# A scan's main loop written out in a fixed order, with POOL's decay operands made one step earlier

## The chip, the cores and the metric

The kernel runs on one core of a Trainium2 chip. The metric is device time in microseconds (us); the time of a kernel is the median of its runs. A profile is one further execution, recorded instruction by instruction; its span is the time from the first to the last recorded instruction.

The engines are named as in the profile: PE multiplies matrices (PEld is its loading of weights), DVE and POOL work elementwise on vectors, ACT applies functions, SP issues the DMAs. Each engine takes its instructions strictly in the order of its own queue; an instruction that waits holds up all that stand behind it on the same engine.

## The reference, cut to what matters

Three parts follow one another: a graph attention, a scan in the manner of Mamba-2, and a feed-forward part with quantized and low-rank weights. The change is in the scan:

```python
h = x * rsqrt(mean(x * x)) * norm_w
proj = einsum('bsd,od->bso', h, in_proj_w)          # gate, hidden, B, C, dt
hBC = silu(causal_conv(hBC, conv_w, conv_b))        # 4 taps along the sequence
hid_dt = hid * dt
M = einsum('bcihn,bcjhn->bcijh', Ch, Bh) * L        # L = exp(segsum(A * dt))
Y_diag = einsum('bcijh,bcjhp->bcihp', M, hid_dt)
y = (Y_diag + D_res) * silu(gate)                   # D_res = Dp * hid
ygr = y * rsqrt(mean over a group of 1024 channels of y * y)
out = residual + einsum('bsd,od->bso', ygr * gnorm_w, out_proj_w)
```

There are 16 sequences of 32 steps (512 tokens), 128 heads of 64 channels (8192 inner channels) and 8 groups. A sequence of 32 fits into one chunk, so that only Y_diag is computed.

## The kernel before, in words

**Tiling.** The 8192 inner channels are 64 tiles `t` of 128 channels, 8 tiles (`TG`) to each of the 8 groups (`G_M`). A tile is 128 channels by 512 tokens, in float32; one matmul of 512 columns shows as two records in the trace.

**The steps of a tile.** `project` (L1181) loads a weight block by a DMA on SP (`win`, 6 buffers) and runs four matmuls into a PSUM tile of a pool with two buffers. For the gate the result is `ppg`, and ACT makes `gs` from it (L1260). For the hidden channels it is `ppch`; `convolve` lets ACT make the first tap `cyh` (L1188), DVE add three taps (L1193), and ACT apply silu to give `hid` (L1196). This is `inner(g)`.

`mix(g)` then takes each tile: PE transposes `hid` into `pht` (L1289); DVE multiplies by `dt` into `hd` (L1291); for every second tile `decays` lets POOL make the operand `da` (L1269), PE sum it into `pl` (L1274) and ACT take the exponential `ed` (L1279); DVE multiplies two `el` (L1302) from `ed` and `CB`; PE multiplies `py` (L1310, 16 records); DVE adds and gates (`hid` L1314, `gs` L1315); ACT squares (`sq`, L1320), POOL adds the squares into `ssq` (L1321), and ACT scales `gs` (L1322).

`close(g)` sums `ssq` on PE (`pn`, L1329), makes the reciprocal root `gr` on ACT and DVE (L70 to L80, L1331), loads eight blocks `wo` of the output weights (L1337) and multiplies them with `gs`: four PSUM tiles `po` of eight matmuls (L1342), in a pool with two buffers; each is scaled and added to `xt` on DVE (L1345).

**Side work.** `lows.load` is a generator of ten chunks for the feed-forward part's low-rank weights: it clears its tiles on POOL (L179), issues nine small DMAs a chunk (L185), and splits a chunk on DVE one step later (`split`, L161 to L173). `inner(g)` for g > 0 takes one step of it after each tile.

**The order.** The source calls `inner(g + 1)`, `mix(g)`, `close(g)`, group by group. But this is not the order in the queues: in the scan a scheduler places the instructions of each engine, and it mixes `close(g)`'s matmuls into those of `mix(g)`, moves most projections of group g + 1 ahead of the mix, and puts ten `wo` loads at the very start of the scan. In the graph part a fixed order of the source holds (`manual_schedule`).

Of the kernel before, what the change touches and what calls it, by code (L numbers as in the profile page):

```python
# [8 lines left out]
F32 = mybir.dt.float32  # L9
# [3 lines left out]
AF = mybir.ActivationFunctionType  # L13
ALU = mybir.AluOpType
# [4 lines left out]
P = 128  # L19
B = 16  # L20
C = 32
D = 512
# [9 lines left out]
CB = 3  # L32
# [8 lines left out]
H_M, G_M, SEQ = 128, 8, 32  # L41
D_INNER = 8192
NT = D_INNER // P
TG = NT // G_M
# [9 lines left out]
def kernel(ctx: ExitStack, tc: tile.TileContext, I, out):  # L54
# [69 lines left out]
    with ExitStack() as cx:  # L124
        scan_part(nc, tc, cx, I, id32, ones, xt, U, rstd, lows)
# [4 lines left out]
class LowRank:  # L130
# [985 lines left out]
def scan_part(nc, tc, cx, I, id32, ones, xt, u, rstd, lows):  # L1116
# [50 lines left out]
    for q in range(4):  # L1167
        pt = ps_m.tile([P, 4, P], F32, tag="m", name=f"pt{q}")
# [6 lines left out]
    def project(t, tag):  # L1175

        w = wpool.tile([P, 4, P], F32, tag="win", name=f"win{tag}", bufs=6)
        nc.sync.dma_start(out=w, in_=I["in_proj"][t])
        pp = ps_p.tile([P, D], F32, tag="p", name=f"pp{tag}")
        for k in range(4):  # L1180
            nc.tensor.matmul(pp, lhsT=w[:, k], rhs=hT[:, k], start=(k == 0), stop=(k == 3))  # L1181
        return pp

    def convolve(dst, t, tag):

        pp = project(NT + t, f"c{tag}")
        y = wk.tile([P, B, SEQ], F32, tag="cy", name=f"cy{tag}", bufs=3)
        nc.scalar.activation(  # L1188
            y.rearrange("p b s -> p (b s)"), pp, AF.Identity, bias=cb[:, t:t + 1], scale=cw[:, t, 3:4]
        )  # L1190
        pv = pp.rearrange("p (b s) -> p b s", b=B)
        for sh in (1, 2, 3):
            nc.vector.scalar_tensor_tensor(  # L1193
                y[:, :, sh:], pv[:, :, :SEQ - sh], cw[:, t, 3 - sh:4 - sh], y[:, :, sh:], ALU.mult, ALU.add
            )
        nc.scalar.activation(dst, y.rearrange("p b s -> p (b s)"), AF.Silu)  # L1196


    wdt = wpool.tile([P, 4, P], F32, tag="win", name="wdt", bufs=6)
# [36 lines left out]
    CB = sc.tile([P, G_M, 4, P], F32, name="CB")  # L1236
# [13 lines left out]
    parts = lows.load(low)  # L1250
    big = cx.enter_context(tc.tile_pool(name="sbig", bufs=2))

    def inner(g):

        gs = big.tile([P, TG, D], F32, tag="gs", name=f"gs{g}")
        hid = big.tile([P, TG, D], F32, tag="hid", name=f"hid{g}")
        for i in range(TG):
            t = g * TG + i
            pg = project(t, f"g{t}")
            nc.scalar.activation(gs[:, i], pg, AF.Silu)  # L1260
            convolve(hid[:, i], t, f"h{t}")
            if g > 0:
                next(parts, None)
        return gs, hid

    def decays(h):

        da = sm.tile([P, 4, 4, SEQ], F32, tag="da", name=f"da{h}", bufs=2)
        nc.gpsimd.tensor_tensor(  # L1269
            da, lei.unsqueeze(1).unsqueeze(1).to_broadcast([P, 4, 4, SEQ]),  # L1270
            dA[:, :, h:h + 4].rearrange("p q h -> p h q").unsqueeze(3).to_broadcast([P, 4, 4, SEQ]), ALU.mult,
        )
        pl = ps_m.tile([P, 4, 4, SEQ], F32, tag="m", name=f"pl{h}")
        nc.tensor.matmul(  # L1274
            pl.rearrange("p h q i -> p (h q i)"), lhsT=gt, rhs=da.rearrange("p h q i -> p (h q i)"),
            start=True, stop=True,
        )
        ed = sm.tile([P, 4, 4, SEQ], F32, tag="ed", name=f"ed{h}", bufs=2)
        nc.scalar.activation(ed, pl, AF.Exp)  # L1279
        return ed  # L1280

    def mix(g, gs, hid):

        ssq = wk.tile([P, D], F32, tag="ssq", name=f"ssq{g}")
        for i in range(TG):
            t = g * TG + i
            pt = ps_m.tile([P, 4, P], F32, tag="m", name=f"pht{t}")
            for q in range(4):
                nc.tensor.transpose(pt[:, q], hid[:, i, q * P:(q + 1) * P], id32)  # L1289
            hd = sm.tile([P, 4, 2, 64], F32, tag="hd", name=f"hd{t}")  # L1290
            nc.vector.tensor_tensor(  # L1291
                hd, pt.rearrange("p q (h c) -> p q h c", h=2),
                dt[:, :, 2 * t:2 * t + 2].unsqueeze(3).to_broadcast([P, 4, 2, 64]), ALU.mult,
            )
            py = ps_y.tile([P, 4, P], F32, tag="y", name=f"py{t}")
            if i % 2 == 0:
                decay = decays(2 * t)
            els = []
            for j in range(2):

                el = sm.tile([P, 4, P], F32, tag="el", name=f"el{2 * t + j}")
                nc.vector.tensor_tensor(  # L1302
                    el.rearrange("p q (b i) -> p q b i", b=4),
                    decay[:, 2 * (i % 2) + j].unsqueeze(2).to_broadcast([P, 4, 4, SEQ]),
                    CB[:, g].rearrange("p q (b i) -> p q b i", b=4), ALU.mult,
                )
                els.append(el)
            for q in range(4):
                for j in range(2):
                    nc.tensor.matmul(  # L1310
                        py[64 * j:64 * j + 64, q], lhsT=hd[:, q, j], rhs=els[j][:, q], start=True, stop=True
                    )
            pyf = py.rearrange("p q t -> p (q t)")
            nc.vector.scalar_tensor_tensor(hid[:, i], hid[:, i], dpc[:, t:t + 1], pyf, ALU.mult, ALU.add)  # L1314
            nc.vector.tensor_tensor(gs[:, i], gs[:, i], hid[:, i], ALU.mult)  # L1315
# [7 lines left out]
        return ssq  # L1323

    def close(g, gs, ssq):
# [8 lines left out]
        wo = []  # L1334
        for i in range(TG):
            w = wpool.tile([P, D], F32, tag="wo", name=f"wo{g}_{i}", bufs=TG + 2)
            nc.sync.dma_start(out=w, in_=I["out_proj"][g * TG + i])  # L1337
            wo.append(w)
        for q in range(4):
            po = ps_o.tile([P, D], F32, tag="o", name=f"po{g}_{q}")  # L1340
            for i in range(TG):
                nc.tensor.matmul(  # L1342
                    po, lhsT=gs[:, i, q * P:(q + 1) * P], rhs=wo[i], start=(i == 0), stop=(i == TG - 1)
                )
            nc.vector.scalar_tensor_tensor(xt[:, q], po, rs[:, q:q + 1], xt[:, q], ALU.mult, ALU.add)  # L1345

    cur = inner(0)
    for g in range(G_M):
        nxt = inner(g + 1) if g + 1 < G_M else None
        ssq = mix(g, *cur)  # L1350
        close(g, cur[0], ssq)
        cur = nxt


def ffn_part(nc, tc, cx, I, id32, xt, layernorm, lows, out):
# [139 lines left out]
```

## Time and profile before

| what | value |
|---|---|
| time, median of 3 runs | 2353.34 us (2352.94 to 2354.5) |
| the profiled execution's own time | 2354.35 us |
| its span | 2352.6 us |
| mean granted TensorE clock | 0.981 |
| first `ppg` matmul | 1402.1 us |
| last `xt` addition of the scan (start) | 2253.48 us |

The main loop of the scan thus lies between 1402 us and 2254 us, 36% of the span. Within it the page's groups give (records, busy time):

| line, engine | what | records | busy us |
|---|---|---|---|
| L1181 PE | `ppg` and `ppch` | 1024 | 464.1 |
| L1342 PE | `po` | 512 | 240.5 |
| L1310 PE | `py` | 1024 | 90.6 |
| L1289 PE | `pht` | 256 | 41.9 |
| L1274 PE | `pl` | 64 | 34.3 |
| L1302 DVE | `el` | 128 | 107.8 |
| L1321 POOL | `ssq` | 56 | 80.1 |

Busy times of PE overlap: a record of 592 ns is followed by the next after 0.43 us. So a group's busy time is not what it adds to the end; that is read from the starts of successive records, in the view in order of time.

### The profile page before, as it was taken

To read this page: it belongs to the slowest core of one execution; us is meant where nothing else is said; L and a number is where in the kernel's file an instruction comes from. 1 tells how busy PE (TensorE), PEld (TensorE's weight loads), DVE (VectorE), ACT (ScalarE), POOL (GpSimd) and SP (SyncE) were. 2 spreads that over 40 slices of the span, in tenths; PEclk is the share of its full clock that TensorE was granted. 3 is DMA by queue.
4 is the path that set the end of the run, shared out by engine and by line. 5 is a ranking of instruction groups with operands and counts; after the bars stand their busy time and mean duration, and the time that the engine had idled before them with its cause. 6 is when DMAs were issued, how large, how long until landed. Compare 5 with 4: busy or idle time off the path is not lost. (4 is left out here: it accounts for less than half of the span.)

```text
span 2352.6 us, 88841 instructions
## 1 busy us (share of the span) xinstructions
PE 2168.6 (92%) x39234; PEld 1240.7 (53%) x39234; DVE 1696.2 (72%) x3674; ACT 1093.0 (46%) x2023; POOL 831.6 (35%) x897
## 2 busy tenths in 40 slices
PE   5598899999999988899999699999999999999979
PEld 2255555776557765577777344444444444444422
DVE  8488897998979999899999658455362635536543
ACT  6686677555765544455555123333242433333321
POOL 2155656555565555655655100011020202112200
PEclk9899999999999999999999799999999999999989
DMA  1324242232232322323111312211212121220000
GB/s 47 72 64 83 49 84 58 56 79 48 64 70 53 82 46 63 74 49 83 41 39 36 105 54 80 68 58 50 76 32 92 34 86 54 59 63 14 28 37 18
DMA packets 121625, 137.99 MB, mean 59 GB/s; under 512 B 18398, under 2 KB 79506, under 8 KB 121154
## 3 DMA queue, kind: packets, MB, share of 16 engines
q1 hardware_dynamic: 121240, 132.32, 22.6%
q8 instruction: 308, 5.05, 0.9%
q14 instruction: 77, 0.63, 0.1%
HBM read 77.02 MB, written 12.85 MB: 38 GB/s over the span
## 5 line engine op out<-in xcount | busy, mean ns | idle before, releaser
L890 POOL TENSOR_TENSOR EN<-e,rz 128x480 f32<-128x480 f32 x344 | 342.3, 995 | 496.7 <-DVE rz L888 405.0
L915 PE MATMUL u<-WA,DD 128*32 128x128 bf16 (+1 forms) x16512 | 411.8, 247 | 18.3 <-issue 17.7
L920 ACT COPY us<-u 128x512 f32<-128x512 f32 x516 | 301.6, 586 | 153.0 <-PE u L915 136.0
L915 PEld LDWEIGHTS <-DD 128*32 128x32 f16 x16512 | 337.2, 97 | 51.8 <-issue 50.4
L811 POOL TENSOR_TENSOR DD<-fs,crep 128x480 f16<-128x480 f32 (+2 forms) x344 | 349.6, 1017 | 0.0
L875 ACT ACTIVATE e<-s,smc 128x480 f32<-128x480 f32 x344 | 227.3, 661 | 252.3 <-PE s L870 220.4
L943 PEld LDWEIGHTS h<-e,us 128*32 128x32 f32 (+1 forms) x11008 | 245.9, 125 | 134.2 <-issue 68.4
L943 PE MATMUL h<-e,us 128*32 128x30 f32 (+1 forms) x11008 | 278.8, 210 | 32.6 <-issue 15.6
L1193 DVE SCALAR_TENSOR_TENSOR cyh<-ppch,t_conv_w,cyh 128x496 f32<-128x496 f32 (+2 forms) x192 | 137.5, 716 | 221.7 <-ACT cyh L1188 217.7
L862 DVE TENSOR_REDUCE c<-s 128x16 bf16<-128x480 f32 x344 | 220.8, 642 | 81.2 <-PE s L853 77.9
L1269 POOL TENSOR_TENSOR da<-lei,dA 128x512 f32<-128x512 f32 x32 | 40.5, 1266 | 612.6 <-PE pl L1274 577.2
L1342 PE MATMUL po<-wo,gs 128*128 128x512 f32 x512 | 240.5, 605 | 10.5 <-DVE xt L1345 10.3
L1181 PE MATMUL ppch<-hT,winch 128*128 128x512 f32 x512 | 232.2, 593 | 0.0
L1181 PE MATMUL ppg<-hT,wing 128*128 128x512 f32 x512 | 231.9, 593 | 0.0
L896 DVE STREAM_TRANSPOSE e<-EN 128x512 f32<-128x512 f32 x344 | 225.2, 655 | 0.0
L882 DVE TENSOR_REDUCE z<-e 128x16 f32<-128x480 f32 x344 | 220.0, 640 | 0.4 <-ACT e L875 0.4
L541 ACT ACTIVATE sgn<-kd 128x512 bf16<-128x512 f32 x256 | 153.1, 598 | 53.0 <-PE kd L540 50.1
L751 DVE TENSOR_SCALAR oh<-it,rank 128x512 bf16<-128x512 f16 x512 | 156.9, 369 | 11.9 <-PE pp L705 11.9
L853 PEld LDWEIGHTS <-DD 128*32 128x32 f16 x5504 | 80.7, 96 | 158.1 <-issue 132.4
L853 PE MATMUL s<-DX,DD 128*32 128x120 f16 x5504 | 141.5, 221 | 19.0 <-DMA DX<-DD 15.3
L1181 PEld LDWEIGHTS ppch<-hT,winch 128*128 128x128 f32 x512 | 93.7, 190 | 122.7 <-issue 122.3
L1181 PEld LDWEIGHTS ppg<-hT,wing 128*128 128x128 f32 x512 | 95.8, 190 | 114.0 <-issue 114.0
(327 smaller groups left out, 2846.0 us busy)
## 6 DMA issues: line engine op xcount, KB each, us to landing
DX<-DD SPq DMA_DIRECT2D x456, 90.0 KB
wo<-in_out_proj SPq DMA_DIRECT2D x64, 256.0 KB
wing<-in_in_proj SPq DMA_DIRECT2D x64, 256.0 KB
winch<-in_in_proj SPq DMA_DIRECT2D x64, 256.0 KB
crep<-dC SPq DMA_DIRECT2D x128, 64.0 KB
dS<-so SPq DMA_DIRECT2D x32, 256.0 KB
fs<-dS SPq DMA_DIRECT2D x128, 64.0 KB
wincB<-in_in_proj SPq DMA_DIRECT2D x8, 256.0 KB
```

The lines of the kernel that those rows point to most:

```text
L811: nc.gpsimd.tensor_tensor(d[:, :, m0 - n0:n1 - n0], win, crep[:, :, m0:n1].unsqueeze(3).to_broadcast([P, 4, n1 - m0, K]), ALU.subtract,)
L853: nc.tensor.matmul(s[rh, j * 4 * QB:(j + 1) * 4 * QB].rearrange("p (b q) -> p b q", b=4), lhsT=d[:, h, c0:c0 + 32], rhs=dx[:, h, :, c0:c0 ...
L862: nc.vector.tensor_reduce(c, live["s", at, gi].rearrange("p (i q) -> p i q", q=QB), AX.X, ALU.max, negate=True)
L875: nc.scalar.activation(e, s.rearrange("p (i q) -> p i q", q=QB), AF.Exp, scale=smc)
L882: nc.vector.tensor_reduce(z, e, AX.X, ALU.add)
L890: nc.gpsimd.tensor_tensor(en[:, :, :QB], e, rz.unsqueeze(2).to_broadcast([P, NI, QB]), ALU.mult)
L896: nc.vector.transpose(e.rearrange("p i q -> p (i q)"), en.rearrange("p i q -> p (i q)"))
L915: nc.tensor.matmul(u[rh, jj], lhsT=d[:, h, c0:c0 + 32], rhs=WA[k][:, h].rearrange("p b o -> p (b o)"), start=(jj == 0 and k == 0), stop=(k ...
L920: nc.scalar.copy(us[:, j - jj:j + 1], u)
L943: nc.tensor.matmul(h[r:r + co, pr, q0:q0 + QB], lhsT=us[:, j, b * co:(b + 1) * co], rhs=e[:, 4 * j + b, :QB], start=npair > 1, stop=True, ...
L1181: nc.tensor.matmul(pp, lhsT=w[:, k], rhs=hT[:, k], start=(k == 0), stop=(k == 3))
L1342: nc.tensor.matmul(po, lhsT=gs[:, i, q * P:(q + 1) * P], rhs=wo[i], start=(i == 0), stop=(i == TG - 1))
```

## The change

From the main loop of the scan on, the source's order is the queues' order (`manual_schedule`), and the source is written anew for it. The parts:

- In each step i of group g: `gate` of tile i of group g + 1; the end of the convolution of tile i - 1 of group g + 1, and after it a step of `lows.load`; `gated` of tile i - 1 of group g; `turn` of tile i (transposes, `hd`, two `el`, and the DMA of that tile's `wo`); the projection and first tap of tile i of group g + 1; `py` of tile i.
- POOL's `da` is made by `spread` in an even step, its sum `pl` and `ed` by `ahead` in the next odd step; both are for the two tiles after that.
- `close(g)` runs as a whole after the mix, `po_0` first, then the sums `pn` and the root, then `po_1` to `po_3`. Only `close(6)` is taken in eight half steps, one inside each step of `mix(7)`, which has no projections.
- `wo` blocks are issued one a step instead of eight a group; `hd` has two buffers instead of three; the other buffer counts are as before.

```diff
-    def inner(g):
...
-    def decays(h):
+    cx.enter_context(tc.manual_schedule())
+    made = {}
+
+    def gate(g, i):
+        if i == 0:
+            made[g] = [big.tile([P, TG, D], F32, tag=n, name=f"{n}{g}") for n in ("gs", "hid")]
+        pg = project(g * TG + i, f"g{g * TG + i}")
+        nc.scalar.activation(made[g][0][:, i], pg, AF.Silu)
+
+    def current(g, i):
+        t = g * TG + i
+        yield from convolve_steps(made[g][1][:, i], t, f"h{t}")
+        if g > 0:
+            next(parts, None)
...
+    def spread(h):
 
         da = sm.tile([P, 4, 4, SEQ], F32, tag="da", name=f"da{h}", bufs=2)
         nc.gpsimd.tensor_tensor(
...
+        summands[h] = da
...
+    def ahead(h):
+        if h < H_M:
+            decay[h] = decays(h)
...
+        def turn(self, i):
+
+            t = self.g * TG + i
             pt = ps_m.tile([P, 4, P], F32, tag="m", name=f"pht{t}")
             for q in range(4):
-                nc.tensor.transpose(pt[:, q], hid[:, i, q * P:(q + 1) * P], id32)
-            hd = sm.tile([P, 4, 2, 64], F32, tag="hd", name=f"hd{t}")
+                nc.tensor.transpose(pt[:, q], self.hid[:, i, q * P:(q + 1) * P], id32)
+            if i % 2:
+                ahead(2 * t + 2)
+            elif 2 * t + 4 < H_M:
+                spread(2 * t + 4)
+            hd = sm.tile([P, 4, 2, 64], F32, tag="hd", name=f"hd{t}", bufs=2)
...
+            w = wpool.tile([P, D], F32, tag="wo", name=f"wo{t}", bufs=TG + 2)
+            nc.sync.dma_start(out=w, in_=I["out_proj"][t])
+            self.wo.append(w)
...
+    def close(g, gs, ssq, wo, pairs):
+
         for q in range(4):
             po = ps_o.tile([P, D], F32, tag="o", name=f"po{g}_{q}")
             for i in range(TG):
                 nc.tensor.matmul(
                     po, lhsT=gs[:, i, q * P:(q + 1) * P], rhs=wo[i], start=(i == 0), stop=(i == TG - 1)
                 )
+                if i == TG // 2 - 1:
+                    yield
+            if q == 0:
+                rs = root(g, ssq)
             nc.vector.scalar_tensor_tensor(xt[:, q], po, rs[:, q:q + 1], xt[:, q], ALU.mult, ALU.add)
+            yield
...
+    for i in range(TG):
+        gate(0, i)
+        end_of(current(0, i))
+    spread(0)
+    ahead(0)
+    last = None
     for g in range(G_M):
-        nxt = inner(g + 1) if g + 1 < G_M else None
-        ssq = mix(g, *cur)
-        close(g, cur[0], ssq)
-        cur = nxt
+        mix = Mix(g)
+        conv = None
+        for i in range(TG):
+            if g + 1 < G_M:
+                gate(g + 1, i)
+            end_of(conv)
+            conv = None
+            if i:
+                mix.gated(i - 1)
+            mix.turn(i)
+            if g + 1 < G_M:
+                conv = current(g + 1, i)
+                next(conv)
+            else:
+                next(last, None)
+            mix.outputs(i)
+        end_of(conv)
+        mix.gated(TG - 1)
+        end_of(last)
+        last = mix.closing()
+        if g + 2 != G_M:
+            end_of(last)
+            last = None
```

`convolve_steps` is `convolve` with a stop after the first tap, so that the taps on DVE and the silu can be queued later. The arithmetic of each step is the same. Counted in the two kernels' queues, ACT loads a function table 40 times more often after the change.

More of the change, by code (lines that the diff above doesn't have):

```diff
@@ L1182, in project, with convolve_steps @@
         return pp
-    def convolve(dst, t, tag):
+    def convolve_steps(dst, t, tag):
         pp = project(NT + t, f"c{tag}")
@@ L1196, in convolve @@
         nc.scalar.activation(dst, y.rearrange("p b s -> p (b s)"), AF.Silu)
+    def convolve(*args):
+        for _ in convolve_steps(*args):
+            pass
     wdt = wpool.tile([P, 4, P], F32, tag="win", name="wdt", bufs=6)
@@ L1251, in scan_part @@
     big = cx.enter_context(tc.tile_pool(name="sbig", bufs=2))
-    def inner(g):
[L1255 to L1264, printed above, removed]
-    def decays(h):
+    cx.enter_context(tc.manual_schedule())
[10 more added lines that the diff above has]
+            next(parts, None)
+    summands = {}
+    def spread(h):
         da = sm.tile([P, 4, 4, SEQ], F32, tag="da", name=f"da{h}", bufs=2)
@@ L1272, in decays @@
         )
+        summands[h] = da
+    def decays(h):
+        da = summands.pop(h)
         pl = ps_m.tile([P, 4, 4, SEQ], F32, tag="m", name=f"pl{h}")
@@ L1280, in decays, with __init__ @@
         return ed
[L1282 to L1286, printed above, removed]
+    decay = {}
+    def ahead(h):
+        if h < H_M:
+            decay[h] = decays(h)
+    class Mix:
+        def __init__(self, g):
+            self.g = g
+            self.gs, self.hid = made.pop(g)
+            self.ssq = wk.tile([P, D], F32, tag="ssq", name=f"ssq{g}")
+            self.wo = []
+            self.pairs = []
+            self.sums = None
+        def turn(self, i):
+            t = self.g * TG + i
             pt = ps_m.tile([P, 4, P], F32, tag="m", name=f"pht{t}")
             for q in range(4):
-                nc.tensor.transpose(pt[:, q], hid[:, i, q * P:(q + 1) * P], id32)
-            hd = sm.tile([P, 4, 2, 64], F32, tag="hd", name=f"hd{t}")
+                nc.tensor.transpose(pt[:, q], self.hid[:, i, q * P:(q + 1) * P], id32)
[4 more added lines that the diff above has]
+            hd = sm.tile([P, 4, 2, 64], F32, tag="hd", name=f"hd{t}", bufs=2)
             nc.vector.tensor_tensor(
@@ L1294, in mix, with outputs @@
             )
-            py = ps_y.tile([P, 4, P], F32, tag="y", name=f"py{t}")
-            if i % 2 == 0:
-                decay = decays(2 * t)
             els = []
+            h0 = 4 * (t // 2)
             for j in range(2):
-                el = sm.tile([P, 4, P], F32, tag="el", name=f"el{2 * t + j}")
+                el = sm.tile([P, 4, P], F32, tag="el", name=f"el{2 * t + j}", bufs=3)
                 nc.vector.tensor_tensor(
                     el.rearrange("p q (b i) -> p q b i", b=4),
-                    decay[:, 2 * (i % 2) + j].unsqueeze(2).to_broadcast([P, 4, 4, SEQ]),
-                    CB[:, g].rearrange("p q (b i) -> p q b i", b=4), ALU.mult,
+                    decay[h0][:, 2 * (i % 2) + j].unsqueeze(2).to_broadcast([P, 4, 4, SEQ]),
+                    CB[:, self.g].rearrange("p q (b i) -> p q b i", b=4), ALU.mult,
                 )
                 els.append(el)
+            if i % 2:
+                decay.pop(h0)
+            self.now = hd, els
+            w = wpool.tile([P, D], F32, tag="wo", name=f"wo{t}", bufs=TG + 2)
+            nc.sync.dma_start(out=w, in_=I["out_proj"][t])
+            self.wo.append(w)
+        def outputs(self, i):
+            t = self.g * TG + i
+            hd, els = self.now
+            py = ps_y.tile([P, 4, P], F32, tag="y", name=f"py{t}")
             for q in range(4):
@@ L1312, in mix, with gated @@
                     )
-            pyf = py.rearrange("p q t -> p (q t)")
+            self.py = py
+        def gated(self, i):
+            t = self.g * TG + i
+            gs, hid, ssq = self.gs, self.hid, self.ssq
+            pyf = self.py.rearrange("p q t -> p (q t)")
             nc.vector.scalar_tensor_tensor(hid[:, i], hid[:, i], dpc[:, t:t + 1], pyf, ALU.mult, ALU.add)
@@ L1322, in mix, with closing, root @@
             nc.scalar.activation(gs[:, i], gs[:, i], AF.Copy, scale=gnw[:, t:t + 1])
-        return ssq
-    def close(g, gs, ssq):
+        def closing(self):
+            return close(self.g, self.gs, self.ssq, self.wo, self.pairs)
+    def root(g, ssq):
         pn = ps_y.tile([P, 4], F32, tag="y", name=f"pn{g}")
@@ L1333, in close @@
         rstd(sm, rs, mean, 4, f"gn{g}")
[L1334 to L1338, printed above, removed]
+        return rs
+    def close(g, gs, ssq, wo, pairs):
         for q in range(4):
@@ L1344, in close, with end_of @@
                 )
+                if i == TG // 2 - 1:
+                    yield
+            if q == 0:
+                rs = root(g, ssq)
             nc.vector.scalar_tensor_tensor(xt[:, q], po, rs[:, q:q + 1], xt[:, q], ALU.mult, ALU.add)
-    cur = inner(0)
-    for g in range(G_M):
-        nxt = inner(g + 1) if g + 1 < G_M else None
-        ssq = mix(g, *cur)
-        close(g, cur[0], ssq)
-        cur = nxt
+            yield
+    def end_of(c):
+        for _ in c or ():
+            pass
+    for i in range(TG):
[4 more added lines that the diff above has]
+    last = None
+    for g in range(G_M):
+        mix = Mix(g)
[21 more added lines that the diff above has]
+            last = None
 def ffn_part(nc, tc, cx, I, id32, xt, layernorm, lows, out):
```

## The prediction

> **What bounds the kernel now.** I read the page first, then the table by stretches, then PE in order of time. Only the scan's main loop (1402.1 to 2253.5 us) is touched.
>
> ```profile
> PE 2168.6 (92%) x39234; PEld 1240.7 (53%) x39234; DVE 1696.2 (72%) x3674; ACT 1093.0 (46%) x2023; POOL 831.6 (35%) x897
> ```
>
> ```profile
> 1800.00:1900.00 100.00, 98.75 (x358) 46.12 (x357) 48.30 (x71) 35.56 (x50) 14.88 (x11) 1.00 0.20 58
> 2200.00:2300.00 100.00, 82.36 (x314) 33.34 (x314) 54.76 (x113) 32.02 (x49) 11.54 (x9) 0.91 0.06 22
> ```
>
> The page gives PE 92% busy over the whole span. Of the stretches, the first is the loop in full run, the second its end (columns: length, busy PE, PEld, DVE, ACT, POOL, granted clock, DMA): in full run PE is busy 98.75%, all others half or less, the clock 1.00; at the end PE falls to 82%. PE is the bound. By busy time only 1% could be had; but busy PE is not PE at its peak, and the starts of its groups tell more:
>
> ```profile
> 1619.69 1.09 PE L1310 MATMUL py<-el,hd 128*64 128x128 f32 x16
> 1620.71 1.09 PE L1289 MATMUL pht<-id,hid 128*128 128x128 f32 x8
> 1621.64 3.60 PE L1181 MATMUL ppg<-hT,wing 128*128 128x512 f32 x8
> 1625.17 1.09 PE L1310 MATMUL py<-el,hd 128*64 128x128 f32 x16
> 1626.20 1.13 PE L1274 MATMUL pl<-da,gt 128*128 128x512 f32 x2
> 1627.16 0.60 PE L1289 MATMUL pht<-id,hid 128*128 128x128 f32 x4
> 1627.60 1.88 PE L1342 MATMUL po<-wo,gs 128*128 128x512 f32 x4
> ...
> 1642.72 1.02 PE L1342 MATMUL po<-wo,gs 128*128 128x512 f32 x2
> 1643.67 0.43 PE L1310 MATMUL py<-el,hd 128*64 128x128 f32 x2
> 1644.04 1.13 PE L1342 MATMUL po<-wo,gs 128*128 128x512 f32 x2
> 1645.20 1.09 PE L1310 MATMUL py<-el,hd 128*64 128x128 f32 x14
> ...
> 1659.25 1.13 PE L1342 MATMUL po<-wo,gs 128*128 128x512 f32 x2 [1.18 <-DVE xt L1345]
> ```
>
> First column: start. Start to start, undisturbed: 16 `py` records take 1.02, `pl` 0.96, four `pht` 0.44, eight projection records 3.53 ahead of `py` (3.43 ahead of another projection: 2136.58 to 2140.01). The lower lines show what the order costs: a `py` tile cut into 2 and 14 records by single `po` matmuls takes 0.95 + 0.37 + 1.16 + 1.02 = 3.50 us where four `po` records (1.72, at 1627.60) and an uncut `py` take 2.74. And the last line: once a group PE waits 1.18 for the root, because the sums `pn` are queued when little of `po_0` and `po_1` is left. That wait ends at 1764.32, 1869.38 and 1974.43 in later groups: the period is 105.06 us.
>
> [...]
>
> **The new PE queue, from these rows.** A tile: `ppg` 3.43, `pht` 0.44, `ppch` 3.53, `py` 1.02: 8.42 us; in odd tiles `pl` 0.96 more. Eight tiles: 8 x 8.42 + 4 x 0.96 = 71.2. A close: 64 records in 13.84 per 32 (`po` 2184.64 to the `pht` at 2198.48), and `pn` 0.92 (2179.72 to 2180.64): 28.6. A period is 99.8, that is 5.3 less for each of the groups.
>
> The whole loop: `inner(0)` 16 x 3.43 = 54.9, a left-over `pcb` 0.9 and the first `pl` 1.0; seven mixes with projections 498.4; closes 0 to 5 171.6; `mix(7)` with `close(6)` inside: 8 x (0.44 + 1.02), 3 x 0.96, 28.6 and 0.1 at each of 8 changes to `py`, 44.0; `close(7)` 28.6. Sum 799.4, against 2253.5 - 1402.1 = 851.4 before. Much of the 52 lies at the end: from 2143.45 to 2253.5 `mix(6)`, `mix(7)` and their closes take 110 us, without projections to fill them.
>
> **Does PE wait in the new order?** All queues go by the source now, so I follow one tile, counted from the end of `ppch`(i-1) as time 0, where PE begins `py`(i-1). ACT's tap 0.2 to 1.0; DVE's three taps (2.23) to 3.2; `hid` and `gs`, 0.66 + 0.60, to 4.5; `hd` needs `pht`(i), done at 1.02 + 3.43 + 0.44 + 0.2 = 5.2, to 5.8; two `el` at 0.60 each to 7.0. PE wants them for `py`(i) at 8.42 (9.38 in odd tiles): 1.4 and 2.4 spare. No wait, as long as POOL does not slow `el`:
>
> ```profile
> 1737.34 1.33 POOL L1269 TENSOR_TENSOR da<-lei,dA 128x512 f32<-128x512 f32 x1
> 1737.67 1.56 DVE L1315 TENSOR_TENSOR gs<-gs,hid 128x512 f32<-128x512 f32 x1
> 1742.03 0.68 DVE L1315 TENSOR_TENSOR gs<-gs,hid 128x512 f32<-128x512 f32 x1
> ```
>
> Beside `da` the same DVE operation takes 1.56, alone 0.68: it ends one own duration after POOL. In the new order `ssq`(i-1) starts near 6.4 (ACT: `gs` 4.65, `hid`, `sq` to 6.4) and lasts 1.47, so the second `el` can be put off to 8.5. I take 2 us for all; the bounds are 0 and both `el` at the worst row (1.75): 5.8 + 3.5 = 9.3, 0.9 in each of 28 even tiles, 25 us.
>
> ACT's 40 more table loads: 1.28 each, 51 us, on an engine busy 36%. In an odd tile: `gs`, `hid`, `sq`, scaling to 7.1, load to 8.4, `ed` 9.0; the next tap is due at 9.5. The load back stands before `gs`, which waits for `ppg` anyway. Cost 0; without that cover the tap and the taps behind it come late by what is over 9.5.
>
> At the close `gs`(7) is ready at 4.5 + 0.63 + 0.72 + 0.2 = 6.1, wanted by the last `po_0` at 1.02 + 7 x 0.86 = 7.0. `ssq` (1.47 after `sq`) is ready at 6.8, wanted at 7.9. From `pn` to the first `xt` takes 3.9 (2180.64 to 2184.55); `po_1` covers it with 6.9. So the 1.18 goes and nothing is late next. In `mix(7)` the root sits in DVE's queue ahead of `gated`(1): 3.9, then 1.26 + 0.6 + 0.6 and steps of 0.6, 7.0, against `py` 1.02, `pht` 0.44 and half of `po_1` 3.5: a new wait of 2.0, once.
>
> Side work: the ten chunks of `lows.load` fell into DVE's idle time of `inner(1)` before (a chunk 3.2 us, 1420.23 to 1423.4). Now each stands in DVE's queue between taps and gating in `mix(0)` and the first tiles of `mix(1)`. DVE's tile becomes 2.23 + 3.2 + 1.26 + 1.8 + 0.88 for one delay by POOL = 9.4 against PE's mean 8.9: 0.5 x 9 = 4.5; `close(0)` waits for `gs`(7) 2.0 (9.1 against 7.1); the masks' ping-pong with POOL 1.0. Together 7.5; bounds 0 and 20 (2 us in each of ten).
>
> SP: `wo` stands before `winch` now, and `wo` of a third tile waits for the end of the close before; six `win` buffers let loads run 2.5 tiles (22 us) ahead, and six blocks landed within 7 us (SP 2192.66, DMA idle again at 2200). Chunk loads wait for the split two chunks back, then 11 issues (3.6) and two blocks: about 12 of the 13.5 us to the use. Cost 0; a late block would cost the difference. In `mix(7)` the last `wo` is free 8 us before its use.
>
> The start of the scan:
>
> ```profile
> 1309.71 2.89 POOL L179 MEMSET lb<- 128x1376 bf16 x3
> 1311.90 2.38 DVE L95 TENSOR_SCALAR n<-h,lnmv_f,lnr_f 128x512 f32<-128x512 f32 x1
> 1319.08 0.55 DVE L95 TENSOR_SCALAR U<-xt,lnmv_s,lnr_s 128x512 f32<-128x512 f32 x1
> ```
>
> POOL's clearing of `lows` held a DVE operation of the chain that leads to the scan's first projections: 2.38 for 0.55. It moves into `mix(0)`: 1.8 gained, 0.5 given back. The ten `wo` loads leave the start, too: 0, since what they delay there is not waited for.
>
> **Sum.** 799.4 + 2 + 2 + 7.5 = 810.9; 851.4 - 810.9 = 40.5, plus 1.3: 41.8. From the profiled 2354.35 that is 2312.5; the median of before is 1.0 lower, so 2311.5, say 2312.
>
> **Rivals.**
> 1. POOL against DVE: the fixed order lets `ssq` and `da` meet both `el` in every even tile, 25 us instead of 2: 2335. For it: 1.56 against 0.68. Against: half the `el` of before took 0.68, and the spare time takes one delay. 0.17. [...]
> 2. Slower than before: the ring of taps, gating, `hd`, `el`, `py` becomes the bound. Beyond 1.4 and 2.4 spare it costs its excess in each of 56 tiles; from 0.74 us a tile (41.8 / 56) the kernel is slower. With each DVE row at its worst, 1.0 + 2.23 + 0.75 + 1.75 + 0.69 + 3.5 = 9.9 against a mean 8.9: 56 us, 2367. Against: three delays a tile need three POOL instructions, and there are 1.5. 0.09.
> 3. It does not do what it says: the cut `py` costs the same uncut, and only PE's waits go (`po` 10.3, `py` 4.9, `pn` 1.3, together 16.5 in the view of waits), less 11.5 of new ones: 2348. Against: the uncut rows above. 0.06.
>
> **How the numbers follow.** The forecast, 2301 (no side-work or POOL cost) to 2324 (side work at its upper bound), has 0.60; below 2301 0.05; 2324 to 2338, mostly the first rival, 0.20; between that and no change 0.06, two thirds of it within 0.2%; slower 0.09. The range 2301 to 2338 leaves out 0.20. A measurement of this kernel can tell about 0.2% (4.7 us) from no change: faster 0.87, same 0.04, slower 0.09.
>
> **What would show it.** Right: PE's period near 100 us, `py` in runs of 16, no `po` waiting for `xt`; in the first mix, tiles of 9.4 us with `py` waiting for `el`; `n` at 0.55. Wrong: PE waiting for `el` in all even tiles (rival 1), or in all tiles (rival 2), or `winch` late at PE.

## The result, and the profile after

The changed kernel takes 2329.19 us (median of 4 runs, 2324.17 to 2334.01), the kernel before in the same comparison 2353.14 (4 runs, 2350.07 to 2354.5): a ratio of 0.990, 95% interval 0.9876 to 0.9924. It is faster, by 24 us where 42 were forecast. The profiled execution took 2327.8 us, its span 2326.1.

The first two lines are from the page, the others from the table by stretches (the columns as before: length, busy PE, PEld, DVE, ACT, POOL, granted clock, DMA):

```profile
PE 2146.4 (92%) x39234; PEld 1243.0 (53%) x39234; DVE 1679.4 (72%) x3674; ACT 1139.2 (49%) x2063; POOL 836.0 (36%) x897
L1368 POOL TENSOR_TENSOR ssq<-ssq,sq 128x512 f32<-128x512 f32 x56 | 88.9, 1588 | 606.5 <-ACT sq L1367 606.5
```

```profile
1800.00:1900.00 100.00, 100.00 (x370) 48.16 (x369) 47.09 (x75) 42.09 (x57) 15.52 (x11) 1.00 0.21 64
2200.00:2300.00 100.00, 83.76 (x204) 26.64 (x203) 36.39 (x88) 24.66 (x38) 0.00 (x0) 0.90 0.06 22
```

PE is still the bound, still 92% busy. In full run its busy share only went from 98.75 to 100.00, yet 370 records lie in the stretch where 358 did. POOL's additions of the squares (`ssq`) take 88.9 us for 80.1 before, in the same 56 instructions. PE in order of time, at the end of a group in full run:

```profile
1837.48 1.02 PE L1288 MATMUL pl<-da,gt 128*128 128x512 f32 x2
1838.34 3.60 PE L1181 MATMUL ppch<-hT,winch 128*128 128x512 f32 x8
1841.87 1.09 PE L1352 MATMUL py<-el,hd 128*64 128x128 f32 x16
1842.89 7.13 PE L1390 MATMUL po<-wo,gs 128*128 128x512 f32 x16
1849.86 0.95 PE L1378 MATMUL pn<-ones,ssq 128*128 128x1 f32 x8
1850.67 20.85 PE L1390 MATMUL po<-wo,gs 128*128 128x512 f32 x48
```

No line has a wait in brackets; `py` is in one piece, and the 48 `po` records behind the sums run through. Five groups in full run begin 100.0 us apart (105.06 before). But the first two are longer, and the trace shows how. PE in the first mix:

```profile
1490.75 1.22 PE L1352 MATMUL py<-el,hd 128*64 128x128 f32 x16
1491.90 3.70 PE L1181 MATMUL ppg<-hT,wing 128*128 128x512 f32 x8
1495.44 0.60 PE L1318 MATMUL pht<-id,hid 128*128 128x128 f32 x4
1495.88 3.60 PE L1181 MATMUL ppch<-hT,winch 128*128 128x512 f32 x8
1499.97 0.43 PE L1352 MATMUL py<-el,hd 128*64 128x128 f32 x2 [0.49 <-DVE el L1333]
1501.64 1.09 PE L1352 MATMUL py<-el,hd 128*64 128x128 f32 x14 [1.24 <-DVE el L1333]
1502.65 5.40 PE L1181 MATMUL ppg<-hT,wing 128*128 128x512 f32 x8
```

`py` waits for both its `el`; the eight `ppg` records behind it take 5.40 instead of 3.70. The table by stretches names the second thing, the granted clock (last column but two):

```profile
1490.00:1500.00 10.00, 9.51 (x39) 4.36 (x37) 8.64 (x17) 5.50 (x8) 0.70 (x2) 1.00 0.23 79
1500.00:1510.00 10.00, 8.76 (x32) 4.37 (x33) 9.48 (x17) 2.73 (x6) 2.65 (x3) 0.83 0.26 82
```

DVE is 95% busy there, and the clock is down to 0.83. Where the forecast's 41.8 us went, from the traces (us):

| stretch | before | forecast | after | forecast missed by |
|---|---|---|---|---|
| a group in full run | 105.06 | 99.8 (+2 in all for POOL) | 100.0 | 1.4 and -2.0 |
| groups 0 and 1 beyond two of 100.0 | - | 7.5 | 12.3 + 5.0 | 9.8 |
| `mix(7)` with `close(6)` inside | - | 44.0 + 2.0 | 52.0 | 6.0 |
| first `ppg` to last `po` of the scan | 850.8 | 40.5 less | 825.7 | 15.4 |
| last `po` to the end | 99.8 | no change | 103.1 | 3.3 |
| last graph matmul to first `ppg` | 94.8 | 1.3 less | 95.1 | 1.6 |

The first three rows are parts of the fourth.

The profiled execution of after is 26.5 us shorter; 5.2 of that is put down to scatter and not to the change: the graph part, which is the same code, ended 5.2 us earlier. Over the thirteen traces of this study its last matmul starts anywhere from 1297.8 to 1308.4, and whole times scatter with it by 5 us and more. So what a few us matter for is read below from the length of a stretch inside the scan, not from the whole time.

### The profile page after: what moved, and what is told of

It is laid out like the page before. It is cut to its first block, busy times and chain, and to the rows that moved or that the text cites. A ratio compares the mean times of both kernels' runs of the same rounds, so it can differ in the third digit from the quotient of the medians.

```text
span 2326.1 us, 88832 instructions
## 1 busy us (share of the span) xinstructions
PE 2146.4 (92%) x39234; PEld 1243.0 (53%) x39234; DVE 1679.4 (72%) x3674; ACT 1139.2 (49%) x2063; POOL 836.0 (36%) x897
## 5 line engine op out<-in xcount | busy, mean ns | idle before, releaser
L915 PE MATMUL u<-WA,DD 128*32 128x128 bf16 (+1 forms) x16512 | 411.7, 247 | 19.3 <-issue 18.7
L1368 POOL TENSOR_TENSOR ssq<-ssq,sq 128x512 f32<-128x512 f32 x56 | 88.9, 1588 | 606.5 <-ACT sq L1367 606.5
L1181 PE MATMUL ppg<-hT,wing 128*128 128x512 f32 x512 | 237.6, 607 | 0.0
L1390 PE MATMUL po<-wo,gs 128*128 128x512 f32 x512 | 226.9, 599 | 2.1 <-ACT gs L1369 2.1
L1265 ACT ACTIVATE gs<-ppg 128x512 f32<-128x512 f32 x64 | 38.1, 595 | 298.4 <-PE ppg L1181 296.9
L1390 PEld LDWEIGHTS po<-wo,gs 128*128 128x128 f32 x512 | 96.7, 192 | 118.7 <-issue 113.2
```

The source lines that it names most:

```text
L915: nc.tensor.matmul(u[rh, jj], lhsT=d[:, h, c0:c0 + 32], rhs=WA[k][:, h].rearrange("p b o -> p (b o)"), start=(jj == 0 and k == 0), stop=(k ...
L1390: nc.tensor.matmul(po, lhsT=gs[:, i, q * P:(q + 1) * P], rhs=wo[i], start=(i == 0), stop=(i == TG - 1))
```

## The experiments

### Where the gain comes from

**Cutting `py` again.** The same instructions; only PE's queue changes:

```diff
         for k in range(4):
+            if k == 3 and between:
+                between()          # the first of py's 8 multiplications
             nc.tensor.matmul(pp, lhsT=w[:, k], rhs=hT[:, k], ...)
...
-            mix.outputs(i)
+            mix.outputs(i, 1, 7)   # the other 7
```

> The changed kernel with the same instructions, but PE's queue cuts every py tile of the seven mixes with projections as the scheduler did: the first py multiplication (2 records) stands ahead of the last ppch multiplication (2 records), the other 14 behind it. Theory, the prediction's step: a cut costs 0.76 us (3.50 against 2.74), in 56 tiles 43 us: the period goes from 100.0 to 106, time 2372 (2360 to 2380). Rival: the cut itself costs nothing or only some 0.1 us a change; what was slow before were PE's waits. Period 100 to 101.5, time 2329 to 2340.

Measured: 2354.14 us, ratio to before 1.0018 (0.9997 to 1.0038), less than the theory's 2360 to 2380, but the whole gain is gone. From the first `ppg` to the last `po` 850.1 us (before 850.8, after 825.7). The period is 104.4, four times alike. One tile of it on PE, and its busy row:

```profile
1709.24 2.74 PE L1183 MATMUL ppch<-hT,winch 128*128 128x512 f32 x6
1711.91 0.43 PE L1357 MATMUL py<-el,hd 128*64 128x128 f32 x2
1712.27 1.13 PE L1183 MATMUL ppch<-hT,winch 128*128 128x512 f32 x2
1713.33 1.09 PE L1357 MATMUL py<-el,hd 128*64 128x128 f32 x14
1714.34 3.70 PE L1183 MATMUL ppg<-hT,wing 128*128 128x512 f32 x8
```

```profile
1800.00:1900.00 100.00, 100.00 (x347) 46.88 (x347) 45.62 (x73) 40.14 (x55) 12.75 (x9) 1.00 0.19 58
```

Start to start, `ppch` and `py` take 1714.34 - 1709.24 = 5.10; uncut 3.53 + 1.02 = 4.55. A cut costs 0.55 (forecast 0.76), eight of them 4.4 a group. PE shows 100.00 busy here as in after, with 347 records for 370: busy time does not see a cut at all. So the theory holds, with a smaller price, and the rival falls. The kernel before had all eight `py` tiles of a group in full run cut, too, as its PE rows show; with the cuts in place the fixed order alone gains 0.6 of 105.06 there.

**`da` at its product.** The second part of the change, undone alone:

```diff
             if i % 2:
+                if 2 * t + 2 < H_M:
+                    spread(2 * t + 2)
                 ahead(2 * t + 2)
-            elif 2 * t + 4 < H_M:
-                spread(2 * t + 4)
```

> The changed kernel with only the second part of the change undone: da is made on POOL in the same odd step as its product pl, not one step ahead. Theory: da then stands on POOL behind ssq of the tile before, ends 9.2 us after the start of the tile (ssq 6.4 to 7.9, da 1.3), and PE, which stands at pl at 4.9 with everything else behind it, waits 4.5 us in each odd tile, and 1.7 more where the clock drops behind the wait: 28 times 4.5 to 6.2, time 2455 to 2503; period 118 to 125. The fixed order would then be slower than before without this part. Rival: POOL has slack enough, or the part is a detail, since its ssq is not waited for: period 100 to 102, time 2329 to 2345.

Measured: ratio 1.055 (1.0525 to 1.0574), 2479.74 us; periods of 118.9 to 119.4. POOL, then PE, in one odd tile:

```profile
1775.64 1.67 POOL L1368 TENSOR_TENSOR ssq<-ssq,sq 128x512 f32<-128x512 f32 x1 [6.85 <-ACT sq L1367]
1777.28 1.07 POOL L1278 TENSOR_TENSOR da<-lei,dA 128x512 f32<-128x512 f32 x1
```

```profile
1773.67 0.60 PE L1318 MATMUL pht<-id,hid 128*128 128x128 f32 x4
1778.40 1.55 PE L1288 MATMUL pl<-da,gt 128*128 128x512 f32 x2 [4.13 <-POOL da L1278]
1779.75 4.91 PE L1181 MATMUL ppch<-hT,winch 128*128 128x512 f32 x8
```

POOL waits 6.85 for the squares with `da` behind them, and PE stands 4.13 at `pl`; the clock falls behind it (`ppch` 4.91 for 3.60; 0.94 granted from 1800 to 1900). The theory holds: a product whose operand is queued behind a late instruction stopped all of PE, 4.13 us in the tile shown. Without this part the change would be 5.5% slower than before.

**`close(6)` apart.**

```diff
-            else:
-                next(last, None)
             mix.outputs(i)
...
-        if g + 2 != G_M:
-            end_of(last)
-            last = None
+        end_of(last)
+        last = None
```

> The changed kernel with close(6) as a whole behind mix(6), instead of in half steps inside mix(7). Theory: much of the gain lies at the end. mix(7) alone is bound by the chain py, gating, hd, two el, py: 4.5 to 5.5 us a tile, 36 to 44 in all, and then 28.6 of close(6), where the interleaved stretch takes 52.0: 13 to 21 us more, time 2342 to 2350. Rival: DVE bounds the interleaved stretch anyway, so that the mixture saves little: 0 to 4 us more, time 2329 to 2333.

Measured: ratio 1.0002 (0.9988 to 1.0015); `mix(7)` takes 45.8 us and `close(6)` 28.5 ahead of it, together 74.3 where the mixture takes 52.0: 22.3 more, a little above the theory's range. The stretch of `mix(7)`:

```profile
2190.00:2220.00 30.00, 17.94 (x100) 11.81 (x100) 20.50 (x25) 7.34 (x12) 8.77 (x6) 0.67 0.00 1
```

PE is 60% busy at a clock of 0.67: it waits for `el` in each tile, and pays twice. The rival, that the mixture saves little, falls.

### Where the first two groups lose

**Side work in the closes.**

```diff
         yield from convolve_steps(made[g][1][:, i], t, f"h{t}")
-        if g > 0:
-            next(parts, None)
...
             nc.vector.scalar_tensor_tensor(xt[:, q], po, rs[:, q:q + 1], xt[:, q], ALU.mult, ALU.add)
+            next(parts, None)
             yield
```

> The changed kernel, with the ten chunks of side work (lows.load) taken out of the tiles' steps and put behind each xt addition of the closes, where DVE has little to do. Theory: the first two groups are slow (112.4 and 104.9 us against 100.0 in full run, 17.3 us together) only because a chunk stands in DVE's queue between taps and gating. Then both groups come to 100 to 101 us, no py waits for an el there, the clock stays at 1.00, and the time falls from 2329 to 2312 (2308 to 2317). Rival 1: the first groups are slow for another reason (first loads of wo, POOL's squares meeting el); groups stay at 112 and 105, time 2325 to 2334. Rival 2: the chunks only carry the wait into the closes (xt late behind a split, po waiting for xt): 1 to 2 us in each of 11 steps, time 2323 to 2334.

Measured: 2313.31 us, ratio 0.9842 (0.9821 to 0.9863); groups 0 and 1 take 102.1 and 102.3. No `py` of theirs waits for `el`. A new wait stands at the end of the closes 0 and 1; PE, and SP's queue ahead of it:

```profile
1551.89 3.70 PE L1181 MATMUL ppg<-hT,wing 128*128 128x512 f32 x8 [1.95 <-DMA wing<-in_in_proj]
```

```profile
1541.22 7.79 SPq L185 DMA_DIRECT2D lw<-in_b1T  x18
1549.11 0.35 SPq L1178 DMA_DIRECT2D wing<-in_in_proj  x1
```

Two chunks' 18 issues, which wait for buffers that DVE has yet to split, hold up the projection's load. So the side work is what the first groups lost by; of this run's rival 2 the place was right and the carrier wrong (SP, not `xt`).

**What makes `el` late?** Taking a chunk from DVE's queue is one thing; which step of the tile is late is another. Four kernels keep the chunks in the mixes. Without POOL's squares:

```diff
-                nc.gpsimd.tensor_tensor(ssq, ssq, sq, ALU.add)
```

> The changed kernel without POOL's additions of the squares for the tiles 1 to 7 of a group; it leaves them out of the sum under the root. The side work stays in the tiles. Theory: in the first group an el pair takes 2.36 us because ssq runs beside it, and this, more than the chunk's own 3.2 us, makes py wait 1.5 us in the even tiles and 2.8 in the second group's. Then the pair takes 1.2, the even tiles come from 10.6 to 9.0 to 9.4, the first two groups to 106 and 102, time 2319 to 2322. Rival: the chunk alone makes DVE late; the pair is faster, but gating and hd are as late, groups 110 to 112 and 104 to 105, time 2325 to 2330. Either way the groups in full run stay at 100.0, since nothing waits for an el there.

Without table loads:

```diff
-        nc.scalar.activation(ed, pl, AF.Exp)
+        nc.scalar.activation(ed, pl, AF.Silu)
```

> The changed kernel with silu in the place of the exponential in ed, so that ACT changes no table in the loop's tiles; it leaves the exponential of the decays out. The chunks stay between taps and gating. Theory: the table load of 1.28 us ahead of ed is what makes the odd tile's tap late in the first group, and the cover that the prediction named for it is gone there. Then DVE no longer waits 1.2 for the tap; two tiles take 19.1 to 19.4 instead of 20.3, the first group 107 to 109 instead of 112.4, the second 103 to 104, time 2321 to 2326; in full run, where the cover holds, the period stays at 100.0. Rival: the loads cost nothing anywhere: 112 and 105 as before, time 2325 to 2331.

The chunk behind the `el` of its step:

```diff
             mix.turn(i)
+            if i and g + 1 < G_M:
+                next(parts, None)
```

> The changed kernel with the chunk of side work moved within the step: behind the two el of a tile, not between taps and gating. The work is the same. Theory: what the prediction left out is ACT. With a chunk ahead of gating, gs comes 3.2 us later, so ACT's sq, scaling, table load and ed come later, and the tap of the odd tile behind them, for which DVE then waits 1.2 us (2.2 without POOL's squares). Behind the el, gating is early again, ACT is free for the tap, and DVE's own work, 8.6 to 9.3 us a tile, is all that is left against PE's 8.9: the first group falls from 112.4 to 100.5 to 105, the second from 104.9 to 100 to 101.5, time 2313 to 2320. Rival: DVE has simply too much work in these tiles, wherever it stands: 110 to 112 and 104 to 105, time 2325 to 2331.

And both of the first two edits together:

> Both of what was taken away singly: no additions of the squares on POOL (left out of the sum under the root) and silu for the exponential of the decays (left out), with the side work in its place. In the first group two tiles took 20.3 us in the changed kernel, 20.3 without the squares, 19.9 without the table loads. Theory: a tile's own chain sets the wait, and POOL's delay of el and ACT's late tap lie beside each other, so that either alone hides behind the other. Without both: tap 1.2 behind the end of ppch, taps 2.1, chunk 3.1, gating 1.4, hd 0.6, two el 1.2, together 9.6 against the 8.9 until PE stands at py: 0.7 of wait in an even tile, two tiles 18.6 to 19.3, the first group 105 to 107.5, the second 101.5 to 103. Rival: another thing holds the tiles (the chunk's loads, PE's clock): two tiles 19.8 to 20.3, the first group 110 to 112.

Measured:

| kernel | two tiles of group 0 | group 0 | group 1 | `mix(7)` | ratio to before |
|---|---|---|---|---|---|
| changed kernel | 20.3 | 112.3 | 105.0 | 52.0 | 0.990 (0.9876 to 0.9924) |
| without squares | 20.3 | 112.4 | 104.1 | 47.1 | 0.988 (0.9855 to 0.9904) |
| without table loads | 19.9 | 110.0 | 102.0 | 52.3 | 0.9892 (0.9864 to 0.992) |
| without both | 18.9 | 105.1 | 101.0 | 47.1 | 0.9832 (0.9796 to 0.9868) |
| chunk behind `el` | - | 108.1 | 100.8 | 51.8 | 0.9882 (0.9866 to 0.9898) |

My first theory for the squares fell: in group 0 their removal gains nothing. DVE in an even tile's chain, first in the changed kernel, then without the squares:

```profile
1491.98 2.22 DVE L1194 SCALAR_TENSOR_TENSOR cyh<-ppch,t_conv_w,cyh 128x496 f32<-128x496 f32 x3 [1.16 <-ACT cyh L1188]
...
1499.23 2.35 DVE L1333 TENSOR_TENSOR el<-ed,CB 128x512 f32<-128x512 f32 x2
```

```profile
1493.35 2.23 DVE L1194 SCALAR_TENSOR_TENSOR cyh<-ppch,t_conv_w,cyh 128x496 f32<-128x496 f32 x3 [2.23 <-ACT cyh L1188]
...
1500.59 1.28 DVE L1333 TENSOR_TENSOR el<-ed,CB 128x512 f32<-128x512 f32 x2
```

And without both:

```profile
1487.60 2.22 DVE L1194 SCALAR_TENSOR_TENSOR cyh<-ppch,t_conv_w,cyh 128x496 f32<-128x496 f32 x3 [0.81 <-ACT cyh L1188]
...
1494.84 1.28 DVE L1333 TENSOR_TENSOR el<-ed,CB 128x512 f32<-128x512 f32 x2
```

The two `el` shrink from 2.35 to 1.28, and the wait for the tap grows from 1.16 to 2.23, as much: the tap is the ACT instruction behind `sq`, scaling, a table load of 1.28 and `ed`, and all of these start late once a chunk stands ahead of gating. Without the squares gating is later still, since POOL's `da` now runs beside it (`gs` on DVE 1.43 for 0.69). The 0.81 that is left without both is the wait for `ppch` and its tap as such. Two delays lie beside each other, and taking away either alone gains little or nothing (20.3 and 19.9 for 20.3); the kernel without table loads thus gains less in group 0 than its theory had (110.0 for 107 to 109). With both gone the pair takes 18.9, inside the range that the tile's own chain gave (18.6 to 19.3). So the chain is the bound, and what is left over PE's 17.9 (two such tiles in full run) is the chunk itself. In full run none of these edits changes the period of 100.0: there POOL and the table loads do lie under PE's work.

The chunk behind `el` moves group 1 to where the theory had it, group 0 only to 108.1. No `py` waits there any more; `ppch` does, for its weights. PE, and SP's queue ahead of it:

```profile
1491.53 3.67 PE L1181 MATMUL ppch<-hT,winch 128*128 128x512 f32 x8 [2.56 <-ACT gs L1367]
```

```profile
1485.91 2.63 SPq L185 DMA_DIRECT2D lw<-in_b1T  x9
1488.63 0.35 SPq L1178 DMA_DIRECT2D winch<-in_in_proj  x1
```

`winch` is issued 2.9 us before `ppch` starts, behind nine issues of a chunk that can begin only when DVE has split the chunk two back, and that is later now. (The `gs` named in brackets is not an input of `ppch`; in two of the later tiles the view names the DMA of `winch`: 0.66 and 1.38.) That part of the theory missed: I followed DVE and ACT, and not SP.

### The clock, the root, and all mends together

**Filling PE's waits.**

```diff
             py = ps_y.tile([P, 4, P], F32, tag="y", name=f"py{t}")
+            for _ in range({(0, 2): 2, (0, 4): 2, (0, 6): 2, (1, 2): 3, (7, 0): 2, (7, 2): 3}.get((self.g, i), 0)):
+                nc.tensor.matmul(
+                    py.rearrange("p q t -> p (q t)"), lhsT=id32, rhs=hT[:, 0], start=True, stop=True
+                )
```

> The changed kernel with extra multiplications by the identity on PE, two or three of 0.86 us each, ahead of those six py tiles that wait for an el (group 0 tiles 2, 4, 6, group 1 tile 2, group 7 tiles 0 and 2); py overwrites what they make. Theory: the half clock of 3.4 us at 1503, 1595 and 2165 comes from the waits of 1.5 to 2.8 us just ahead of it, PE having been idle. With PE kept busy these three drops go and the granted clock is 1.00 there, while the waits are filled; the one at 1544, behind close(0)'s wait, which has no filling, stays. Time 2324 to 2328, that is 1 to 5 us less although PE does 11 us more work. Rival: the drops come from something else (heat, what PE did long before); they stay, and the time is 0 to 5 us longer.

Measured: ratio 0.9889 (0.986 to 0.9917), and all drops of the clock inside the loop are gone. PE and the clock at the place shown above:

```profile
1495.77 1.88 PE L1351 MATMUL py<-hT,id 128*128 128x512 f32 x4
1497.58 1.61 PE L1356 MATMUL py<-el,hd 128*64 128x128 f32 x16
1499.12 3.70 PE L1181 MATMUL ppg<-hT,wing 128*128 128x512 f32 x8
```

```profile
1500.00:1510.00 10.00, 10.00 (x40) 4.89 (x39) 8.61 (x16) 6.26 (x8) 1.45 (x1) 1.00 0.27 82
```

With 14 extra multiplications, 12 us of PE's time, group 0 takes 109.3 for 112.3, group 1 103.4 for 105.0, `mix(7)` 50.3 for 52.0, 6.2 us less in all. The drops at the filled places come from the waits, and the rival falls there. This rests on one trace, but the drop in group 1 stands in both other traces with the same unfilled tiles, and that in `mix(7)` in all four; the one in group 0 stands in no other, so that its absence shows little. One point went against the theory: the drop behind `close(0)`'s unfilled wait of 2.13 is gone too. Why is open (last section).

**The root in two steps.**

```diff
-        rstd(sm, rs, mean, 4, f"gn{g}")
-        return rs
+        steps = rstd.steps(sm, rs, mean, 4, f"gn{g}")
+        next(steps)                # logarithm and exponential on ACT
+        return rs, steps
...
-                rs = root(g, ssq)
+                rs, steps = root(g, ssq)
+                if g + 2 == G_M:
+                    yield
+                end_of(steps)
```

> The changed kernel with the root of close(6), inside mix(7), cut in two: its mean, logarithm and exponential in one step, the rest and the first xt a step later, so that DVE gates tile 1 while ACT loads its tables. Theory: this removes the waits of py in tile 2 of mix(7) (1.42 + 1.18, with a half clock of 3.4 us behind): the stretch from the end of mix(6) to the end of close(6), 52.0 us, falls to 47.5 to 49, time 2324 to 2326. Rival: DVE's own work, el beside ssq, bounds this stretch: 51 to 52, time 2328 to 2330.

Measured: `mix(7)` 48.45 for 52.02, as the theory had it, and no drop of the clock there; the whole time, 2328.54 (6 runs, 2321.32 to 2334.33; ratio 0.9898, 0.9876 to 0.9921), scatters by more than these 3.6 us. In the changed kernel the place is this:

```profile
2157.24 3.60 PE L1390 MATMUL po<-wo,gs 128*128 128x512 f32 x8
2162.26 0.40 PE L1352 MATMUL py<-el,hd 128*64 128x128 f32 x2 [1.42 <-DVE el L1333]
2163.84 1.09 PE L1352 MATMUL py<-el,hd 128*64 128x128 f32 x14 [1.18 <-DVE el L1333]
2164.85 1.03 PE L1318 MATMUL pht<-id,hid 128*128 128x128 f32 x4
2165.68 1.91 PE L1288 MATMUL pl<-da,gt 128*128 128x512 f32 x2
```

**All mends.** Beside the root in two steps: two chunks a close (`if q < 2: next(parts, None)`), and in the feed-forward part

```diff
-    for q in range(4):
-        layernorm(sm, v[:, q], xt[:, q], f"ff{q}")
+    for q in range(4):
+        ...                        # bn_stats and bn_aggr into mvs[:, q]
+    rstd(sm, rr, mvs[:, :, 1], 4, "ff")
+    for q in range(4):
+        nc.vector.tensor_scalar(v[:, q], xt[:, q], mvs[:, q, 0:1], rr[:, q:q + 1], ALU.subtract, ALU.mult)
```

> All mends together: side work in the closes (two chunks a close, behind the first two xt additions, so that its loads don't stand ahead of wing on SP), the root of close(6) cut in two, and the four layernorms of the feed-forward part with one reciprocal root of four columns (two table loads instead of eight). Theory: 12 to 16 us from the first groups, 3 to 4 from mix(7), 6.7 from the layernorms (statistics 2.6, tables and functions 3.0, rest 3.0 against 15.5 from the last xt to the last v): 2329 less 22 to 27, 2302 to 2307, 2.0% under the kernel before. Rival: the mends don't add, since what was late is replaced by the next wait (DVE in mix(7), wing late behind the closes): 2309 to 2318.

Measured: 2298.99 us, ratio 0.9784 (0.9761 to 0.9808), a little under the theory's range. Groups 0 to 5 all take 100.0, `mix(7)` 48.4, and from the last `po` to the end 96.4 for 103.1, 6.7 less as forecast. ACT behind the last `xt`, in this kernel:

```profile
2212.56 1.28 ACT L72 ACT_TABLE_LOAD   x1 [22.37 <-issue]
2213.85 0.20 ACT L72 ACTIVATE rss_ff<-rst_ff 128x4 f32<-128x4 f32 x1
2214.08 1.28 ACT L74 ACT_TABLE_LOAD   x1
2215.37 0.20 ACT L74 ACTIVATE rsr_ff<-rss_ff 128x4 f32<-128x4 f32 x1
```

The changed kernel loads eight tables there (from 2226.34 to 2236.94), the kernel before only six (from 2256.46 to 2264.22), because the scheduler, which still orders the feed-forward part, had put the logarithms of two quarters behind one load there and their exponentials behind another. From the first load to the end of the last function that is 12.1 us for 9.3, or 2.8 of the 3.3 us by which this part, in no line of the diff, grew. One root of four columns needs two loads.

## Why the prediction was right or wrong, point by point

- **PE is the bound, by what its order costs.** Right. Put the cuts back and the gain is gone (850.1 of 850.8). A cut was sized at 0.76 and measures 0.55.
- **A period of 99.8.** Right: 100.0. It was summed from undisturbed rows, so that the wrong size of a cut did not enter it. Busy time does not tell the two orders apart: PE is 100.00 busy at periods of 104.4 and of 100.0.
- **Tables on ACT, 0; `close` covers the root; SP 0.** Right in full run: without table loads the period is the same 100.0, and no `po` waits for `xt` and no `ppg` or `ppch` for its weights. The condition that stood beside it, "without that cover the tap and the taps behind it come late", is what happens in group 0 (a wait of 1.16 for the tap).
- **POOL's delay of `el`, 2 us in all; rival 1.** In full run it costs 0 (100.0 with and without squares), and rival 1 falls. The meeting itself is there (an `el` pair of 2.35 beside `ssq`, 1.28 without; in the prediction's row of before `gs` ends 0.56 behind the end of `da`, and takes 0.68 alone), but spare time takes it. It does cost where there is none: 4.9 us in `mix(7)` (52.0 to 47.1), where the prediction had nothing for it.
- **Side work 7.5.** This step failed; it cost 17.3. The prediction added the chunk to DVE's total ("9.4 against PE's mean 8.9: 0.5 x 9 = 4.5"), as if DVE could work ahead. But its own chain gave the answer: gating done at 4.5 is done at 7.7 behind a chunk of 3.2, `hd` and two `el` (1.8) end at 9.5, and with the one delay by POOL (0.88) at 10.4, against the 8.42 at which PE wants them in an even tile: 2.0 late, where these tiles of group 0 measure 2.0 to 2.2. Gating is late for ACT as well. DVE can't work ahead, because the taps wait for a `ppch` that PE makes only after the `py` before. From start to start on PE, waits of `py` measure 9.9 in both groups against 4.5; `close(0)`'s wait 2.4, near the forecast (2.0); the masks nothing (1.0 forecast); and half clock, three steps, 5.1, which was not foreseen. Without squares and table loads the two groups cost 6.1 over two of 100.0. The bounds of 0 to 20 held the 17.3.
- **`mix(7)` 44.0 + 2.0.** The wait behind the root was named at the right place, but is larger with the clock behind it: 3.6 (52.02 to 48.45 with the root in two steps). Without the squares the stretch is 47.1, 1.1 over the forecast: `el` beside `ssq` is 4.9 of the 6.0. The two shares overlap, since without the squares there is no drop of the clock behind the root either, and no run takes away both.
- **Start of the scan 1.3.** `n` takes 0.54 for 2.38, and `pd` starts 14.9 us behind the last graph matmul for 16.2: 1.3, as summed. By the first `ppg` it is given back in this trace (95.1 against 94.8; the other traces of the new order have 92.6 to 95.1). Why it varies was not tried.
- **The end.** Forecast unchanged, measured 3.3 longer, of which 2.8 by two more table loads that a scheduler placed.
- **Rival 2** (the ring bound in all tiles) falls: it binds only where a chunk stands in it. **Rival 3** (a cut costs nothing) falls by the cut put back.

So three terms of the sum were mis-sized for a reason that the runs show: side work, `mix(7)` and the feed-forward part, 9.8 + 6.0 + 3.3 = 19.1 us of the 20.5 between the 41.8 forecast and the 21.3 (26.5 less the graph part's 5.2) that the change itself gave in the profiled execution. The 2329.19 lies inside the stated 2301 to 2338, but in the part above 2324 that was kept mostly for rival 1, and these three terms brought it there in its place: that the range held is in part luck.

## What to carry to other kernels

In a fixed order, cost an inserted piece of work along the latency chain of one step, from the instruction that starts it to the one that waits for it, not by the engine's sum of busy time; side work belongs where its engine has no one waiting, and its DMA issues where nothing is queued behind them (here `wing` stood behind 18 of them, and PE waited 1.95). If two delays end at the same wait, taking one away can show next to nothing (here 20.3 and 19.9 for 20.3): take both (18.9). And keep a matrix engine's short runs whole: a cut that no busy time shows cost 4% of each group here.

## What the runs showed of the hardware

The granted clock falls in steps of 3.41 us on a grid that runs through the whole trace, and by half: in the changed kernel it is 0.50 from 1502.8 to 1506.2 us and 1.00 on both sides, and in the traces of before and after all its changes lie whole multiples of 3.413 us apart. `po` and `ppg` records begin 0.85 us apart at 0.50 instead of 0.43. I summed the time in which PE stands idle in each such step of the scan's main loop in all thirteen traces, for the 148 steps at full clock with over 0.3 us of it. Of the 74 with under 1.4 us, none was followed by a step at half clock; of the 31 with over 2.2, all were (24 of them in the kernel that makes `da` at its product); of the 43 between, 14. So waits of some 2 us cost up to 1.7 more here (5.40 for 3.70 above), and 3.4 where the half clock lasts two steps, as behind `close(0)` in three traces (in the kernel with the root in two steps 25.98 from the `po` behind the wait to the end of the last `po`, in the filled one 22.62). Between 1.4 and 2.2 the sum alone does not decide: in the kernel without table loads a wait of 1.54 was followed by a drop in one even tile of group 0 and not in the next, and of the wait in `close(0)` 1.86 lay in one step of the grid in the changed kernel, with a drop, and 2.00 with the filling, without one. What else counts is open.
